# Weight buffers of an expert layer: eight in place of four, and the loads of the early tiles moved to its start

## The chip, the cores and the metric

The kernel runs on one core of one Trainium2 chip. The metric is the device time of one execution in microseconds (us), the median of several runs. A difference of 0.2%, about 4 us here, is about the smallest that these runs can tell from none.

## The reference, cut to what matters

Two transformer-like layers work on 4096 tokens of width D = 256, each an attention-like part and a mixture of experts, each with a residual and a layer norm:

```python
x = _layernorm(x + _L0_attn_ref(...))   # three recurrent (RG-LRU) layers
x = _layernorm(x + _L0_ffn_ref(x, Wg, W1, W2))   # 8 experts, each token goes to one
x = _layernorm(x + _L1_attn_ref(...))   # attention, 16 heads, 512 tokens a row
x = _layernorm(x + _L1_ffn_ref(...))   # 16 experts, each token goes to four
```

The change is in the second line, whose expert part is

```python
cap = max(1, T // E)                       # T = 4096, E = 8, cap = 512
_, top_idx = jax.lax.top_k(pT, cap)        # each expert takes its 512 best tokens
...
for e in range(E):
    gate = jnp.where(tok2exp == e, weights, 0.0)
    h = jax.nn.gelu(xt @ W1[e], approximate=False) @ W2[e]
    out = out + gate[:, None] * h
```

W1 is 256 x 512 and W2 512 x 256 for each expert, all in float32.

## The kernel before, in words

**Stages.** `block` (L1846) runs the recurrent layers, the first expert layer (`expert_choice_layer`, L1119), the attention (`attention_layer`, L1522) and the second expert layer (`token_choice_layer`, L1789) one after the other. A scheduler places the instructions of each engine, except in regions marked `manual_schedule`, where the named engines keep the order of the program.

**The first expert layer.** Each token's row is written to the list of its expert in device memory (`m0rows`) by an indirect DMA from POOL, 128 rows at a time (`put`, L729, L731). The lists are cut into tiles of 128 rows, which are worked one by one: 39 tiles, a number that covers every way in which the tokens may fall. The first eight, the early tiles (`NE0` = 8, L47), are full tiles made from the first half of the tokens. They need only the first half of the list writes: POOL issues 19 of its 32 writes, then a fence (`fence`, L746, a memset at L749 that waits for 16 of them), then the gathers of the eight early tiles (`gather`, L878, L882), with the remaining writes between them.

A table in SBUF (`table`, L770) tells for each tile where its rows start, which expert's weights it needs, and whether the expert differs from that of the table's entry before. Tiles t, t+4, t+8 and so on are given adjacent entries of the table (`entry`, L841), so that they mostly share an expert. SP reads these entries into registers (`value`, L849, L851).

**Weights.** One tile's weights are one DMA of 128 x 2068 floats, 1034 KB (`weights`, L920). The kernel has NW = 4 weight buffers, and tile t uses buffer t % 4. Tiles 0 to 3, and 8 to 11 (the first four of the second table), are loaded without a condition (L925). All others are conditional DMAs (L927), which move nothing if the buffer already holds the right expert. A load into a buffer waits until PE is done with the buffer's last tile.

**The tile loop of `run` (L898).** For tile t, `turn` transposes the rows on PE (L943) and copies them on DVE (L945); `first` multiplies by W1 on PE (L956) with the gelu on ACT (L964); `second` multiplies by W2 on PE (L978), after which DVE adds the residual (L1202) and POOL scatters the rows to `res` (L1205), two scatters under way at most. After `second(t-1)` SP loads the rows of tile t+3 (L935) and then its weights. In this layer SP and POOL keep the order of the program; PE, ACT and DVE don't have to.

SP's order at the start is: the weights of tiles 0 to 3 (L985); eight DMAs that end the lists (`end_list`, L758, L765); the table entries of tiles 4 to 7, read ahead (L989); nothing for the rows of tiles 0 to 7, which were gathered; the weights of tile 4, 5, 6 and 7, one in each turn of the loop; the rows and weights of tile 8, and so on. The rows of tile 8 need all list writes (`L.close`, L1196). At the end of the layer eight DMAs bring `res` back to SBUF (L1224), once the last scatters have landed.

**What follows.** The attention begins with a layer norm (L59 and following) of those eight parts, transposes (L143), the values V (L1566, with the weights `wv`, loaded at L1548) and their bias (L1587, with the table `bt`, loaded at L1550). Its pools of SBUF reuse the bytes of the expert layer's released pools; a pool is given by default to wait for every user of a released pool on whose bytes it lands.

The second expert layer uses the same class, with `bias` True; there the number of buffers and the order of the loads stay as they are.

Of the kernel before, what the change touches and what calls it, by code (L numbers as in the profile page):

```python
# [10 lines left out]
F32 = mybir.dt.float32  # L11
# [6 lines left out]
P = 128  # L18
# [29 lines left out]
NW = 4  # L48
G1 = S // P
WPK = DC * F + FC * D + FC + E1  # L50
# [636 lines left out]
class Lists:  # L687
# [82 lines left out]
    def table(self, n, up, t0, done=None):  # L770

        nc, rp, E, nm = self.nc, self.rp, self.E, f"{self.name}_{t0}"
        tab = rp.tile([P, 4], I32, name=f"tab{nm}")
        self.tabs.append((t0, tab))
        nb_i = rp.tile([P, E], I32, name=f"nb_i{nm}")
        nb = rp.tile([P, E], F32, name=f"nb{nm}")
        cum = rp.tile([P, E], F32, name=f"cum{nm}")
        le = rp.tile([P, E], F32, name=f"le{nm}")  # L780
        et = rp.tile([P, 2], F32, name=f"et{nm}")
        blk = rp.tile([P, 1], F32, name=f"blk{nm}")
        more = rp.tile([P, 1], F32, name=f"more{nm}")
        self.nb, self.cum = nb, cum

        def blocks():
            nc.vector.tensor_scalar_add(nb_i, n, float(up))
            nc.vector.tensor_single_scalar(nb_i, nb_i, 7, ALU.logical_shift_right)
            nc.vector.tensor_copy(nb, nb_i)
            if done is not None:  # L790
                nc.vector.tensor_sub(nb, nb, done)

        def ends():
            nc.vector.tensor_tensor_scan(cum, self.ones[:, :E], nb, 0.0, ALU.mult, ALU.add)
            nc.vector.tensor_scalar(
                le, cum, self.pnw, None, ALU.is_le, ALU.add, accum_out=et[:, 1:2]
            )
            nc.vector.tensor_scalar(
                le, cum, self.pno, None, ALU.is_le, ALU.add, accum_out=et[:, 0:1]
            )  # L800

        def block():
            nc.vector.scalar_tensor_tensor(le, le, 1.0, nb, ALU.mult, ALU.mult, accum_out=blk)
            nc.vector.tensor_sub(blk, self.pno, blk)
            if done is not None:
                nc.vector.tensor_scalar(le, self.iot, et[:, 0:1], None, ALU.is_equal)
                nc.vector.scalar_tensor_tensor(
                    le, le, 1.0, done, ALU.mult, ALU.mult, accum_out=more
                )
                nc.vector.tensor_add(blk, blk, more)  # L810

        def entries():
            nc.vector.tensor_scalar_mul(blk, blk, float(P))
            nc.vector.scalar_tensor_tensor(blk, et[:, 0:1], float(LT), blk, ALU.mult, ALU.add)
            nc.vector.tensor_scalar_min(tab[:, 0:1], blk, float(E * LT))
            nc.vector.tensor_scalar(
                tab[:, 1:2], et[:, 0:1], float(P), float(E * P - P), ALU.mult, ALU.min
            )

            nc.vector.tensor_tensor(tab[:, 2:3], et[:, 0:1], et[:, 1:2], ALU.not_equal)  # L820

        return [(0.8, blocks), (0.7, ends), (0.6, block), (0.8, entries)]
# [26 lines left out]
    def value(self, t, n, hi):  # L849
        i, tab = self.entry(t), self.of(t)[1]  # L850
        return self.nc.values_load_multi_w_load_instructions(  # L851
            tab[i : i + 1, n : n + 1],
            engines=[mybir.EngineType.SP], min_val=0, max_val=hi,
            skip_runtime_bounds_check_because="clamped where the table is made",
        )[1][0]
# [32 lines left out]
    def weights_of(self, t, w_pack):  # L888
        at = self.value(t, 1, self.E * P - P)
        return w_pack.rearrange("e p f -> (e p) f")[bass.ds(at, P), :]  # L890
# [7 lines left out]
    def run(self, ctx, ident, w_pack, bias, done, taken=None, besides=None):  # L898

        tc, nc, E, NT, nm = self.tc, self.nc, self.E, self.NT, self.name
        table, value, weights_of = self.of, self.value, self.weights_of
        wp = ctx.enter_context(tc.tile_pool(name=f"{nm}w", bufs=1))
        hp = self.hp
        psX = ctx.enter_context(tc.tile_pool(name=f"{nm}psX", bufs=2, space=PSUM))
        psH = ctx.enter_context(tc.tile_pool(name=f"{nm}psH", bufs=4, space=PSUM))
        psO = ctx.enter_context(
            tc.tile_pool(name=f"{nm}psO", bufs=1 if bias else 2, space=PSUM)
        )  # L910
        ws = [None] * len(self.held) + [
            wp.tile([P, WPK], F32, name=f"{nm}ws{i}") for i in range(len(self.held), NW)
        ]
        ws[: len(self.held)] = self.held
        xgs, hTs, read = {}, {}, {}

        def known(t):
            return weights_of(t, w_pack), None if t - table(t)[0] < NW else value(t, 2, 1)

        def weights(t):  # L920
            if t < len(self.held):
                return
            w, differs = read.pop(t, None) or known(t)
            if differs is None:
                nc.sync.dma_start(ws[t % NW], w)  # L925
            else:
                nc.sync.dma_start(ws[t % NW], w, cond=differs)  # L927

        def load(t):
            if t in self.got:  # L930
                xgs[t] = self.got.pop(t)
                return
            xgs[t] = hp.tile([P, RW], F32, tag="xg", bufs=NW + 1, name=f"{nm}xg_{t}")
            at = value(t, 0, E * LT)
            ins = nc.sync.dma_start(xgs[t], self.rows[bass.ds(at, P), :]).ins  # L935
            if t < self.early:
                self.reads(ins)

        def turn(t):
            xg = xgs[t]  # L940
            ps = psX.tile([P, DC, P], F32, tag="x", name=f"{nm}xp_{t}")
            for dc in range(DC):
                nc.tensor.transpose(ps[:, dc, :], xg[:, dc * P : (dc + 1) * P], ident)  # L943
            xq = hp.tile([P, DC, P], F32, tag="xq", name=f"{nm}xq_{t}")
            nc.vector.tensor_copy(xq, ps)  # L945
            xgs[t] = (xg, xq)

        def first(t):
            xg, xq = xgs[t]
            w = ws[t % NW]  # L950
            hT = hp.tile([P, FC, P], F32, tag="hT", name=f"{nm}hT_{t}")
            for fc in range(FC):
                ps = psH.tile([P, P], F32, tag="h", name=f"{nm}h_{t}_{fc}")
                for dc in range(DC):
                    o = dc * F + fc * P
                    nc.tensor.matmul(  # L956
                        ps, w[:, o : o + P], xq[:, dc, :],
                        start=(dc == 0), stop=(dc == DC - 1),
                    )
                o = DC * F + FC * D + fc  # L960
                if bias:
                    ins = nc.scalar.activation(hT[:, fc, :], ps, AF.Gelu, bias=w[:, o : o + 1])  # L962
                else:
                    ins = nc.scalar.activation(hT[:, fc, :], ps, AF.Gelu)  # L964
            hTs[t] = hT
            if taken:
                taken(t, xg, w)
                xgs[t] = None, None
            return ins.ins

        def second(t):
            xg, _ = xgs.pop(t)
            hT = hTs.pop(t)
            w = ws[t % NW]
            ps = psO.tile([P, D], F32, tag="o", name=f"{nm}o_{t}")
            for fc in range(FC):
                o = DC * F + fc * D
                nc.tensor.matmul(  # L978
                    ps, hT[:, fc, :], w[:, o : o + D], start=(fc == 0), stop=(fc == FC - 1)
                )  # L980
            done(t, xg, ps)


        for t in range(0 if bias else NW):
            weights(t)  # L985
        if besides:
            besides(-1, None)

        read.update({t: known(t) for t in range(NW, 0 if bias else self.early)})  # L989
        for t in range(NW):  # L990
            load(t)
            if bias:
                weights(t)
        turn(0)
        for t in range(NT + 1):
            if t < NT:
                ins = first(t)
            if t + 1 < NT:
                turn(t + 1)
            if t > 0:  # L1000
                second(t - 1)
                if t + NW - 1 < NT:
                    load(t + NW - 1)
                    weights(t + NW - 1)
            if besides and t < NT:
                besides(t, ins)

# [951 lines left out]
```

## Time and profile before

| What | Value |
|---|---|
| Timed runs (3) | median 1981.51 us, 1978.31 to 1982.03 |
| Profiled execution | 1997.18 us, of which 1995.4 us span |
| Granted TensorE clock, mean of the span | 0.928 |
| PE busy | 1738.8 us (87%) |
| DVE, ACT, POOL busy | 1131.7, 1003.7, 523.9 us |
| First expert layer: first weight load issued, last matmul over | 472.4 us, 665.7 us |
| Weight loads issued in it | 39, 1034 KB each |
| Early tiles' gathers issued by POOL | 495.5 to 515.2 us |

The profile is of one execution, and times in it count from its span's start. In a timeline a row is one instruction or a merged run of them: start, length, engine, line, what is written and read, how many; in brackets how long the engine sat idle before it and what ended that. PE is the matmul row of TensorE, PEld its weight loads, SPq the DMA issues of SyncE. A row of DMA_DIRECT2D has the issue's length on its engine, not that of the transfer.

### The profile page before, as it was taken

What the parts mean: (1) busy time and instruction counts of PE and PEld (TensorE: products, weight loads), DVE (VectorE), ACT (ScalarE), POOL (GpSimd) and SP (SyncE); (2) the same over time, 40 slices, a digit from 0 to 9 for tenths busy, and PEclk for the clock granted to TensorE, in tenths of its full rate; (3) what the DMA queues carried; (4) which work ended last, traced back from release to release, by engine and by line L of the source; (5) the groups of instructions that cost most, each with busy time, mean ns of one, the idle gap of its engine ahead of it and who ended that gap; (6) DMA issues with size and microseconds to landing.
All of it is one profiled execution on the core that took longest, in us unless ns stands there. A gap on an engine that the chain in (4) does not pass through costs nothing. (4 is left out here: it accounts for less than half of the span.)

```text
span 1995.4 us, 31137 instructions
## 1 busy us (share of the span) xinstructions
PE 1738.8 (87%) x10398; PEld 1137.1 (57%) x10398; DVE 1131.7 (57%) x2844; ACT 1003.7 (50%) x2166; POOL 523.9 (26%) x447
## 2 busy tenths in 40 slices
PE   7999995531799698898989998987999999999995
PEld 3555553321699585222222222323889999999994
DVE  6999998853122541676877786884434222222226
ACT  4899976400123331357666766655534334343343
POOL 1000000004422221001041323243666644444440
PEclk8999998655799897899999999998999999999998
DMA  9990000004554300000010111122676767566558
GB/s 358 399 390 1 1 0 1 32 7 166 178 187 147 121 1 17 16 17 17 16 59 17 59 34 43 43 84 73 162 211 130 152 158 186 110 145 139 118 103 255
DMA packets 115262, 217.10 MB, mean 109 GB/s; under 512 B 17101, under 2 KB 85919, under 8 KB 108320
## 3 DMA queue, kind: packets, MB, share of 16 engines
q1 hardware_dynamic: 81536, 165.77, 25.3%
q0 software_dynamic: 30560, 46.72, 11.8%
q10 hardware_dynamic: 3008, 2.63, 0.4%
q8 instruction: 84, 1.38, 0.3%
q14 instruction: 74, 0.61, 0.1%
HBM read 244.79 MB, written 100.43 MB: 173 GB/s over the span
## 5 line engine op out<-in xcount | busy, mean ns | idle before, releaser
L1758 DVE TENSOR_REDUCE nmx<-s 128x1 f32<-128x512 f32 x512 | 330.0, 686 | 157.9 <-PE t L1680 98.7
L1765 ACT ACTIVATE pe<-t 128x512 f32<-128x512 f32 x512 | 277.8, 594 | 206.7 <-PE t L1680 195.0
L1668 PE MATMUL s<-kT,qT 32*128 32x512 f32 x1024 | 302.8, 665 | 54.2 <-ACT pe L1765 25.6
L1680 PE MATMUL t<-qA,kT 32*128 32x512 f32 x1024 | 291.3, 645 | 2.5 <-ACT pe L1765 2.0
L1817 POOL DMA_INDIRECT acc<-y,at x143 | 221.7, 1550 | 260.0 <-DVE at L1810 192.5
L1668 PEld LDWEIGHTS s<-kT,qT 32*128 32x128 f32 x1024 | 81.6, 189 | 219.7 <-ACT pe L1765 174.5
L962 ACT ACTIVATE m1hT<-m1h,m1ws 128x128 f32<-128x128 f32 x284 | 103.9, 368 | 154.9 <-PE m1h L956 133.9
L962 ACT ACTIVATE m1hT<-m1h,xT 128x128 f32<-128x128 f32 x288 | 105.6, 368 | 148.8 <-PE m1h L956 131.5
L1816 DVE TENSOR_SCALAR y<-m1o,gt 128x256 f32<-128x256 f32 x143 | 69.1, 483 | 169.6 <-PE m1o L978 163.2
L945 DVE COPY m1xq<-m1xp 128x256 f32<-128x256 f32 x143 | 60.6, 424 | 180.2 <-PE m1h L956 87.8
L731 POOL DMA_INDIRECT m1rows<-x_ext,slot x128 | 127.0, 992 | 114.5 <-ACT pe L1765 74.8
L956 PE MATMUL m1h<-m1xq,xT 128*128 128x128 f32 x1152 | 143.4, 278 | 4.6 <-issue 2.9
L956 PEld LDWEIGHTS m1h<-m1xq,xT 128*128 128x128 f32 x1152 | 141.2, 194 | 9.3 <-issue 3.8
L956 PEld LDWEIGHTS m1h<-m1xq,m1ws 128*128 128x128 f32 x1136 | 137.4, 192 | 7.0 <-issue 3.5
L956 PE MATMUL m1h<-m1xq,m1ws 128*128 128x128 f32 x1136 | 138.7, 275 | 2.4 <-DVE m1xq L945 2.3
L978 PE MATMUL m1o<-xT,m1hT 128*128 128x256 f32 x576 | 138.4, 382 | 0.7 <-issue 0.5
L1704 PE MATMUL po<-pe,V 128*17 128x512 f32 x1024 | 136.4, 605 | 1.2 <-ACT pe L1765 1.2
L978 PE MATMUL m1o<-m1ws,m1hT 128*128 128x256 f32 x568 | 134.9, 379 | 0.0
L1734 POOL TENSOR_TENSOR AO<-AO,on 128x256 f32<-128x256 f32 x32 | 23.5, 735 | 352.6 <-DVE on L1729 335.0
L964 ACT ACTIVATE m0hT<-m0h 128x128 f32<-128x128 f32 x156 | 43.2, 278 | 143.8 <-PE m0h L956 117.6
L978 PEld LDWEIGHTS m1o<-xT,m1hT 128*128 128x128 f32 x576 | 104.3, 192 | 12.3 <-ACT m1hT L962 0.7
L978 PEld LDWEIGHTS m1o<-m1ws,m1hT 128*128 128x128 f32 x568 | 102.2, 190 | 10.8
(358 smaller groups left out, 3005.7 us busy)
## 6 DMA issues: line engine op xcount, KB each, us to landing
xT<-in_w_pack SPq DMA_DIRECT2D x72, 1034.0 KB
m1ws<-in_w_pack SPq DMA_DIRECT2D x71, 1034.0 KB
m0ws<-in_w_pack SPq DMA_DIRECT2D x39, 1034.0 KB
m0rows<-zero SPq DMA_DIRECT2D x5, 6360.0 KB
m1xg<-m1rows SPq DMA_DIRECT2D x143, 138.0 KB
acc<-zero SPq DMA_DIRECT2D x2, 4096.0 KB
f<-acc SPq DMA_DIRECT2D x16, 512.0 KB
m0rows<-zero SPq DMA_DIRECT2D x1, 4770.0 KB
```

What stands on the lines that cost most here:

```text
L731: ins = self.nc.gpsimd.indirect_dma_start(out=self.rows[:, :], out_offset=bass.IndirectOffsetOnAxis(ap=place, axis=0), in_=row, in_offset= ...
L945: nc.vector.tensor_copy(xq, ps)
L956: nc.tensor.matmul(ps, w[:, o : o + P], xq[:, dc, :], start=(dc == 0), stop=(dc == DC - 1),)
L962: ins = nc.scalar.activation(hT[:, fc, :], ps, AF.Gelu, bias=w[:, o : o + 1])
L978: nc.tensor.matmul(ps, hT[:, fc, :], w[:, o : o + D], start=(fc == 0), stop=(fc == FC - 1))
L1668: mm = nc.tensor.matmul(ps, qTs[u % NR][r, qc * P : (qc + 1) * P], kTs[u % NR][r, :], start=True, stop=True,)
L1680: mm = nc.tensor.matmul(ps, kTs[v % NR][r, kc * P : (kc + 1) * P], qAs[v][r, :], start=True, stop=True,)
L1704: mm = nc.tensor.matmul(po[h4 * HP : h4 * HP + VW, :], V[:, b * NQ + kc, 4 * g + h4, :], pes.pop((u, kc, h4)), start=(kc == 0), stop=(kc = ...
L1758: ins = nc.vector.tensor_reduce(at, ps, AX.X, ALU.max, negate=True)
L1765: ins = nc.scalar.activation(pe, ps, AF.Exp)
L1816: nc.vector.tensor_scalar_mul(y, ps, gt)
L1817: nc.gpsimd.indirect_dma_start(out=R.acc[t % 2][:, :], out_offset=bass.IndirectOffsetOnAxis(ap=at, axis=0), in_=y, in_offset=None, compute ...
```

## The change

For this layer the number of weight buffers becomes eight, the number of early tiles. Tile t up to 7 has buffer t; from tile 8 on it is t % 4 as before. The weights of tiles 4 to 7 are loaded without a condition, right behind the DMAs that end the lists, ahead of the loop; in the loop the loads begin with tile 8. Their read-ahead of conditions goes away. The second expert layer keeps four buffers.

```diff
         ws = [None] * len(self.held) + [
-            wp.tile([P, WPK], F32, name=f"{nm}ws{i}") for i in range(len(self.held), NW)
+            wp.tile([P, WPK], F32, name=f"{nm}ws{i}")
+            for i in range(len(self.held), NW if bias else self.early)
         ]
...
-        xgs, hTs, read = {}, {}, {}
+        xgs, hTs = {}, {}
+
+        many = 0 if bias else self.early
+        at = lambda t: t if t < many else t % NW
 
         def known(t):
-            return weights_of(t, w_pack), None if t - table(t)[0] < NW else value(t, 2, 1)
+            return weights_of(t, w_pack), None if t < many or t - table(t)[0] < NW else value(t, 2, 1)
 
         def weights(t):
             if t < len(self.held):
                 return
-            w, differs = read.pop(t, None) or known(t)
+            w, differs = known(t)
             if differs is None:
-                nc.sync.dma_start(ws[t % NW], w)
+                nc.sync.dma_start(ws[at(t)], w)
             else:
-                nc.sync.dma_start(ws[t % NW], w, cond=differs)
+                nc.sync.dma_start(ws[at(t)], w, cond=differs)
...
-            w = ws[t % NW]
+            w = ws[at(t)]
...
         if besides:
             besides(-1, None)
-
-        read.update({t: known(t) for t in range(NW, 0 if bias else self.early)})
+        for t in range(NW, many):
+            weights(t)
         for t in range(NW):
             load(t)
...
                 if t + NW - 1 < NT:
                     load(t + NW - 1)
-                    weights(t + NW - 1)
+                    if t + NW - 1 >= many:
+                        weights(t + NW - 1)
```

More of the change, by code (lines that the diff above doesn't have):

```diff
@@ L973, in second @@
             hT = hTs.pop(t)
-            w = ws[t % NW]
+            w = ws[at(t)]
             ps = psO.tile([P, D], F32, tag="o", name=f"{nm}o_{t}")
```

## The prediction

> **What bounds the kernel now.** The page's chain that ended last covers only the tail, so I read the first expert layer (472 to 668 us of the profiled execution) by itself, first as a table of stages. Columns after the stretch: its length, busy us (count) of PE, PEld, DVE, ACT and POOL, granted TensorE clock, DMA share, GB/s.
>
> ```profile
> 476.00:492.00 16.00, 0.00 (x0) 0.00 (x0) 0.00 (x0) 1.28 (x1) 12.35 (x13) 0.50 1.03 390
> 492.00:496.00 4.00, 0.00 (x0) 0.00 (x0) 0.00 (x0) 0.00 (x0) 0.63 (x3) 0.50 0.62 181
> 496.00:516.00 20.00, 14.63 (x72) 12.86 (x72) 1.27 (x3) 2.22 (x8) 15.43 (x16) 0.69 0.33 106
> 516.00:528.00 12.00, 0.72 (x3) 0.75 (x4) 1.30 (x3) 1.00 (x4) 6.32 (x8) 0.60 0.51 170
> ...
> 536.00:556.00 20.00, 20.00 (x143) 18.97 (x143) 4.10 (x10) 6.57 (x24) 4.99 (x6) 1.00 0.96 351
> 556.00:664.00 108.00, 108.00 (x753) 102.02 (x753) 26.35 (x58) 32.02 (x116) 29.23 (x30) 1.00 0.42 136
> 664.00:668.00 4.00, 1.73 (x8) 1.17 (x7) 0.97 (x2) 1.56 (x2) 0.97 (x1) 1.00 0.09 33
> ...
> 672.00:684.00 12.00, 6.03 (x17) 4.30 (x18) 7.88 (x34) 5.63 (x12) 0.00 (x0) 0.50 1.05 333
> ```
>
> From 536 to 664 PE is never idle at full clock: tiles 4 to 38 are bound by TensorE, and no weight load is late for it. Time can only change ahead of that (the head, 472 to 536) or behind it (the hand-over to attention, 664 to 700). Next, the timeline of the head (start, length, engine, line; idle time before and its releaser in brackets):
>
> ```profile
> 491.10 0.98 POOL L731 DMA_INDIRECT m0rows<-x_ext,slot  x1 [0.30 <-issue]
> 494.66 0.10 POOL L749 MEMSET m0full<- 128x1 f32 x1 [2.58 <-DMA m0rows<-x_ext,slot]
> 495.54 1.05 POOL L882 DMA_INDIRECT m0got<-m0rows,at  x1 [0.78 <-POOL m0full L749]
> ...
> 498.62 0.66 PE L943 MATMUL m0xp<-ident,m0got 128*128 128x128 f32 x2 [25.48 <-DMA m0got<-m0rows,at]
> ...
> 516.11 19.81 SPq L927 DMA_DIRECT2D m0ws<-in_w_pack  x4
> ...
> 527.28 3.75 PE L956 MATMUL m0h<-m0xq,m0ws 128*128 128x128 f32 x16 [11.36 <-ACT m0hT L964]
> ```
>
> The layer starts when the last list write ahead of the fence lands (494.66) and then the first gather (498.6): two small transfers in series. Weights of tiles 0 to 3 were issued at 472.4 to 475.6 and are not what PE waits for. The four conditional loads of tiles 4 to 7 go out only at 516.1 to 535.9; the waits of SP say why (total, times, longest):
>
> ```profile
> SPq L927 <- PE m0o L978: 21.3, 1, 21.3
> ```
>
> That 21.3 us is SP waiting for tile 0's buffer, with nothing behind it that PE needs: first(4) starts at 535.83, when tile 4's weights (issued 516.11) are long there, and PE is busy without a break from 528. It is a long wait that costs nothing.
>
> **The change part by part.** (1) Removed: four reads of the condition on SP (the eight reads of that moment have a median of 0.60 us) and SP's wait. SP is not late here, so 0; if it were, 4 x 0.6 = 2.4 us.
>
> (2) Moved: the loads of tiles 4 to 7 go from 516 to 536 to right behind the eight end-of-list writes (SP is done with those at 489.5), so about 490.5 to 494. In before one of the four was skipped: of the four issues the shortest took 113 ns against 333 to 359 for the others, the time of an issue that moves nothing. So the change moves 4 x 1034 KB = 4.24 MB at once, 1.06 MB of it new. At 390 GB/s less what POOL's own list writes take (138 KB per 1.28 us, 110 GB/s) that is 280 GB/s, some 15 us: the DMA stays full until about 506, where before it fell to a share of 0.62 at 492 and 0.33 from 496. Into exactly that stretch fall the last list writes, the fence and the first gathers.
>
> What does a full queue cost a small indirect transfer? Two rows of the same kind, a tile's 128 KB scatter:
>
> ```profile
> 534.40 0.97 POOL L1205 DMA_INDIRECT res<-z,m0got  x1 [5.58 <-DVE z L1202]
> ...
> 541.17 0.97 POOL L1205 DMA_INDIRECT res<-z,m0got  x1 [3.73 <-DMA res<-z,m0got]
> ...
> 666.53 0.97 POOL L1205 DMA_INDIRECT res<-z,m0xg  x1 [2.54 <-DVE z L1202]
> 668.93 7.48 SPq L1224 DMA_DIRECT2D x_ext<-res  x8
> ```
>
> The scatter at 541.17 waits for the one two before it, issued at 534.40: 6.8 us with weights in the queue. The last one (666.53) releases SP at 668.93: 2.4 us with the queue empty. So a full queue adds 4.4 us. In the head the gather took 498.5 - 495.5 = 3.0 us, so up to 3.8 more; the last list write took 3.56 us, partly under load already, so up to 3.2 more. Upper bound 7.0 us; lower bound 0 (more bytes in the queue can't make a write land sooner). The Trainium skill (DMA: Bandwidth & Descriptors, Queues, rings and completion order) says that each DMA engine takes turns between its queues packet by packet. By that rule a 138 KB transfer still gets half of 390 GB/s and loses only 0.35 us, 0.7 us for the two; by the scatter's row it is 7.0. The row is of this kernel, but had two weight loads and a backlog ahead; I take +1.5 for the fence and +2.5 for the gather, **+4**. All of it moves PE's start and nothing later absorbs it, since PE is the bound from then on.
>
> (3) Buffers: tiles 8 to 11 now reuse buffers 0 to 3, free long before, so their loads need only the fence at 537.3 and no longer tile 4 to 7. PE was not waiting (20.00 of 20.00 busy at 536 to 556), so 0.
>
> (4) Bytes of SBUF, which the diff doesn't show. In the program before, the weight pool lies at bytes 134,080 to 167,216 of each partition (8,288 a buffer); eight buffers end at 200,368. The attention layer's `wv` (from 176,160) and `bt` (to 188,448) then lie on buffers 5 and 6. All tiles of a pool wait for every user of the released pools on whose bytes it lands. Before, those two loads were clear of the layer and ran ahead of it:
>
> ```profile
> L1548 SPq DMA_DIRECT2D wv<-in_Wv x1: 380/380/380, 391.8 to 391.8; - x1
> ...
> L1550 SPq DMA_DIRECT2D bt<-in_bt x1: 467/467/467, 392.2 to 392.2; - x1
> ```
>
> while `wq` and `wk`, which do lie on the layer's bytes, went out at 684. After, `wv` and `bt` (256 + 1280 KB = 1.57 MB) must wait for tile 38's last matmul (663.83 + 1.89 = 665.7). SP is then idle until 668.93, so I expect them at once, ahead of the eight `x_ext<-res` loads. 1.57 MB at 333 to 390 GB/s is 4.0 to 4.7 us. The idle DMA of 665.7 to 668.9 (share 0.09) hides 3.2 us of it, leaving 0.8 to 1.5; but the last scatter, which gates the res loads, now shares a full queue (0 to +4.4 us). From 672 to 684 the DMA is full (1.05), so a delay there is passed on to the first layer norm at 673.26 and to PE behind it. Bounds +0.8 and +5.9; with the transfer's 1 and about a fifth of the scatter's 4.4, **+2**. A gain from their absence at 391 is excluded: the gates then wait for the end of the recurrent layers (402.9), not for a DMA.
>
> Sum: 0 + 4 + 0 + 2 = +6 us on the profiled execution's own 1997.18 (span 1995.4 and 1.8 around it). The timed runs have a median of 1981.51, 15.7 us shorter; the profile's PE gaps at 508 to 527 (2.1 and 11.4 us, ended late although the work ahead was recorded as done) may be longer in it than in timed runs. They contain no wait for weights, so the sum doesn't use them: 1981.5 + 6 = **1987.5 us**.
>
> **The rivals.** *Faster: the gap at 516 to 527 is the load's doing.* Tile 4's load, issued at 516.11, fills the DMA (share 0.81 at 516 to 520) just when the last gathers and list writes are under way, and PE resumes only at 527. With the load gone from there PE could resume earlier by between the load's own 4.7 us (1.06 MB at the 224 GB/s of 516 to 520) and the whole gap of 11.4; I take 6, and 2 back for the hand-over: 1977.5. It decides from the point where the gap shrinks by more than the two small delays, 6 us. Against it: PE's instruction there waits for ACT, not for a DMA, and the gap outlasts the load. *No change: the loads are hidden.* The share of 0.33 at 496 to 516 has room for them, the skill's rule holds (+0.7), and the hand-over costs 0.8 to 2: 1983.5. *Worse: SP's order.* If `wv` and `bt` come behind `krow` (685.0), V's first matmul moves from 680.1 to about 688; PE then has 43 busy us to do in a stretch of 47, so 5 to 8 us are lost instead of 2: 1992.
>
> **How the numbers follow.** The likeliest case, both small delays (1983 to 1990), has 0.53; SP's order 0.11; no change 0.21; faster 0.15. Differences within 0.2% (4 us: 1977.5 to 1985.5) are what a measurement of this kernel can't tell from none. Slower than that: 0.49 of the likeliest and SP's 0.11, together 0.60; same: the 0.21, 0.04 of the likeliest and 0.05 of the faster case, 0.30; faster by more, 0.10. The range reaches about to the middle of the faster case, 1978, and past SP's order with the upper bounds of both delays, 1995.
>
> **What would show it.** Right: four weight issues at 490 to 495; a DMA share near 1 until about 505; fence at 496, first gather's data for PE at 502 to 503; the same 3.8 us a tile from then on; `wv` and `bt` at 666, `x_ext<-res` at 670, first layer norm at 675. Wrong: PE's first matmul still at 498.6 (then the skill's rule holds); PE's gap at 516 to 527 gone or longer; `wv` still at 391.

## The result and the profile after

The kernel before has a median of 1980.45 us (20 runs, 1973.89 to 1984.64), the changed one 1988.78 us (20 runs, 1981.81 to 1993.1). The ratio is 1.0034, with a 95% interval of 1.0024 to 1.0044: 6.7 us slower (4.8 to 8.7). The two medians by themselves are 8.3 us apart; the ratio, which has the interval, is used from here on. The profiled execution after took 1992.7 us (span 1990.9). It can't be set against the profiled 1997.18 us of before: that one lies far outside the runs that it was shown with (1978.31 to 1982.03), and the section on the experiments comes back to it.

The table of stages of after, columns as in the prediction:

```profile
492.00:496.00 4.00, 0.00 (x0) 0.00 (x0) 0.00 (x0) 0.00 (x0) 0.06 (x1) 0.50 1.09 230
496.00:516.00 20.00, 11.67 (x73) 10.90 (x74) 2.18 (x5) 3.33 (x12) 14.56 (x16) 0.70 0.78 302
516.00:528.00 12.00, 12.00 (x84) 11.23 (x83) 3.45 (x8) 3.34 (x12) 8.66 (x10) 1.00 0.34 115
```

The DMA share of 492 to 516 has risen from 0.62 and 0.33 to 1.09 and 0.78: the four loads are there. PE begins later (11.67 us busy in the 20 us instead of 14.63), but the gap of 516 to 528, where PE had 0.72 us of work in 12, is gone. That last difference isn't the change's doing, as the experiments will show. The timeline of the head of after:

```profile
490.22 3.62 SPq L929 DMA_DIRECT2D m0ws<-in_w_pack  x4
496.39 0.10 POOL L749 MEMSET m0full<- 128x1 f32 x1 [4.34 <-DMA m0rows<-x_ext,slot]
497.27 1.05 POOL L882 DMA_INDIRECT m0got<-m0rows,at  x1 [0.78 <-POOL m0full L749]
...
503.48 0.66 PE L947 MATMUL m0xp<-ident,m0got 128*128 128x128 f32 x2 [30.33 <-DMA m0got<-m0rows,at]
```

The fence comes 1.7 us later than before (494.66), and the gather takes 503.5 - 497.3 = 6.2 us instead of 3.1. PE starts 4.9 us later. The hand-over to attention in the timeline of after:

```profile
651.66 1.89 PE L982 MATMUL m0o<-m0ws,m0hT 128*128 128x256 f32 x8
...
653.58 0.40 SPq L1553 DMA_DIRECT2D wv<-in_Wv  x1
654.02 0.46 SPq L1555 DMA_DIRECT2D bt<-in_bt  x1
654.35 0.97 POOL L1210 DMA_INDIRECT res<-z,m0xg  x1 [2.54 <-DVE z L1207]
660.04 6.95 SPq L1229 DMA_DIRECT2D x_ext<-res  x8
...
664.12 1.41 DVE L59 BATCH_NORM_STATS2 st_m<-x_ext 128x6 f32<-128x256 f32 x4 [3.50 <-DMA x_ext<-res]
...
668.61 2.17 PE L143 MATMUL tp<-ident,x_ext 128*128 128x128 f32 x8 [15.07 <-ACT x_ext L68]
```

`wv` and `bt` have moved from 391.8 to right behind tile 38's last matmul (653.55). The last scatter shares the DMA with them and needs 660.04 - 654.35 = 5.7 us instead of 2.4 until it releases SP. From the last matmul to the first layer norm it is 10.6 us instead of 7.5, and PE's idle time ahead of the first attention transposes (the bracket of the last row) is 15.07 us. Before it was this:

```profile
677.40 2.17 PE L143 MATMUL tp<-ident,x_ext 128*128 128x128 f32 x8 [11.67 <-ACT x_ext L68]
```

### The profile page after: what moved, and what is told of

Its sections match the earlier page's. It is cut to its first block, busy times and chain, and to the rows that moved or that the text cites. A ratio compares the mean times of both kernels' runs of the same rounds, so it can differ in the third digit from the quotient of the medians.

```text
span 1990.9 us, 31138 instructions
## 1 busy us (share of the span) xinstructions
PE 1741.2 (87%) x10398; PEld 1136.8 (57%) x10398; DVE 1130.9 (57%) x2844; ACT 1003.8 (50%) x2166; POOL 523.5 (26%) x447
## 4 chain that ended last, share of the span: by engine, by line
PE 54%; DVE 4%; ACT 4%; issue 2%; POOL 1%; DMA 1%; SPq 0%; ACTq 0%; POOLq 0%; DVEq 0%
PE s L1673 13%; PE m1h L960 13%; PE m1o L982 12%; PE po L1709 5%; PE qk L1645 3%; PE bv L1592 2%; DVE nmx L1763 2%; ACT pe L1770 2%; PE m1xp L947 2%; PE v L1571 1%; PE t L1685 1%; ACT L99 1%; ACT L98 1%; DVE st_m L59 1%; DMA acc<-y,at 0%
```

## The experiments

Theory A is the prediction's: a delay of PE's start (4 to 5 us) and one of the hand-over (2 to 3) add up. Rivals: B, all in the head; C, all in the hand-over; D, the extra megabyte, the missing condition or the order of the instructions.

**Each place undone, and one alone.** `tail_undone` moves the attention's small pool clear of the eight buffers:

```diff
+            pad = pre.enter_context(tc.tile_pool(name="avpad", bufs=1))
+            hole = pad.tile([P, 6144], F32, name="hole")
             vp = pre.enter_context(tc.tile_pool(name="av", bufs=1))
```

> The change, with a hole of 24,576 bytes ahead of the attention layer's pool for wv and bt, so that they lie behind the eight buffers (from byte 200,736) and are loaded at 391 us again. Theory A (both places): the head's delay stays, the hand-over's goes: 4 to 5 us over the kernel before, 2 to 3 under the change; in the profile wv at 391, the last scatter landing 2.4 us after its issue, first gather's data still 6 us after its issue. Rival B (all of the loss in the head): 7 us over the kernel before. Rival C (all in the hand-over): 0. Rival D (the 1.06 MB and the eight buffers themselves): 7.

`tail_alone` is the kernel before with eight buffers reserved, of which it uses four:

```diff
-            wp.tile([P, WPK], F32, name=f"{nm}ws{i}") for i in range(len(self.held), NW)
+            wp.tile([P, WPK], F32, name=f"{nm}ws{i}")
+            for i in range(len(self.held), NW if bias else self.early)
```

> The kernel before, with eight buffers reserved of which four stay unused, so that only the bytes move: wv and bt have to wait for the layer's last matmul, and every weight load is as before. Theory A: 2 to 3 us over the kernel before, the last scatter landing about 5.7 us after its issue instead of 2.4. Rival B: 0. Rival C: 7. Rival D: 0 if it is the megabyte.

`head_undone` is the change with the early loads behind the first rows; `both_undone` has the hole as well:

```diff
-                nc.sync.dma_start(ws[at(t)], w)
+                ins = nc.sync.dma_start(ws[at(t)], w).ins
+                if t == NW and not bias:
+                    tc.add_manual_dep(ins, self.gathers[NW - 1].name, SYNC, reason="rows first")
```

> The change, with tile 4's load held on SP until the fourth gather has landed (5 to 7 behind it): all four unconditional and early, but behind the first rows; the hand-over as in the change. Theory A: the fence at 494.7 and PE's first transpose at 498.6 again, 2 to 3 us over the kernel before, 4 to 5 under the change. Rival B: 0 over before. Rival C: 7 over before. Rival D: 7 over before.

> Both of these together: eight buffers and four unconditional loads stay, but they are issued behind the fourth gather, and wv and bt lie clear of the layer. Theory A, B and C: the time of the kernel before within 1.5 us. Rival D (the extra megabyte, the missing condition, or the order of the instructions): 7 us over it still.

Measured against the kernel before on the same chip (median 1993.38 us there), with the 95% interval: `tail_undone` 1.0003 (0.9990 to 1.0015), +0.6 us; `tail_alone` 1.0041 (1.0028 to 1.0053), +8.2; `head_undone` 1.0036 (1.0026 to 1.0046), +7.2; `both_undone` 1.0007 (0.9992 to 1.0022), +1.4. On this chip that is rival C: moving the bytes alone costs all of the loss, and undoing the head brings nothing. D falls, since `both_undone` keeps the megabyte, the missing condition and the order. In the timeline of `tail_alone`, where no weight load differs from before:

```profile
664.63 0.40 SPq L1548 DMA_DIRECT2D wv<-in_Wv  x1
665.08 0.46 SPq L1550 DMA_DIRECT2D bt<-in_bt  x1
665.40 0.97 POOL L1205 DMA_INDIRECT res<-z,m0xg  x1 [2.54 <-DVE z L1202]
...
672.69 0.33 POOL L723 MEMSET m1none<- 128x276 f32 x1 [6.32 <-DMA res<-z,m0xg]
...
681.27 2.17 PE L143 MATMUL tp<-ident,x_ext 128*128 128x128 f32 x8 [16.68 <-ACT x_ext L68]
```

The scatter takes 7.2 us, and PE's idle time is 16.68 us, 5.0 more than before. But in `tail_undone` the head is as late as in after (first transposes at 502.61), and the time is that of before. Where does the head's delay go?

**PE's gap.** PE's start moved by 4 us and the end of its gap didn't: PE is back for good at 528.14 in `tail_undone`, at 527.28 in before. In the gap it waits for ACT, and ACT for PE's results. The waits of ACT from 496 to 530, in before (total us, times, longest):

```profile
ACT m0hT L964 <- PE m0h L956: 28.9, 7, 24.1
ACT m0hT L964 <- remote: 17.3, 4, 11.0
```

"Remote" is a wait that no recorded end of work explains. Two rows of before show the longest of them:

```profile
510.28 2.46 PE L956 MATMUL m0h<-m0xq,m0ws 128*128 128x128 f32 x16 [2.09 <-ACT m0hT L964]
...
521.01 0.28 ACT L964 ACTIVATE m0hT<-m0h 128x128 f32<-128x128 f32 x1 [11.02 <-remote]
```

PE's matmuls by W1 are over at 512.7, and ACT begins its gelu of them only at 521.0, 8.3 us later. All this time POOL issues list writes and gathers back to back. Theory E: the gap ends with POOL's stream, whenever PE began, so the head's delay is lost in it. `after_again` is the change itself on another chip of this kind. `lists_first` moves POOL's later list writes ahead of the first gather, so PE starts much later and has less of the stream beside it:

```diff
-            put(NC // 2 + 3)
+            put(left)
             L.grown = L.fence(NC // 2)
             for t in range(NE0):
                 L.gather(t)
-                if t >= NW - 1:
-                    put(min(left, 2))
-            put(left)
```

> The change itself, on the chip of the four runs before. Theory A (head and hand-over add up): 7 us by the hand-over and 4 to 5 by the head, 11 to 12 over the kernel before. Theory E (on this chip PE has a gap of about 13 us in the first tiles, which ends with POOL's list writes whenever PE began, so that the head's delay is lost in it): 6 to 8 us, all of the hand-over; in the profile PE starts at 503 but is at tile 10 at the time of the kernel before, within 1.5 us.

> The kernel before, with POOL's 13 later list writes put ahead of the first gather: weights, conditions and bytes as before; PE's first tile starts 13 x 1.3 = 17 us later. Theory E: PE runs with no gap then, and 13.5 of the 17 us are regained: 2 to 5 us over the kernel before. Theory A (a delay of PE's start is a delay of the layer): 17 us over.

Against the kernel before (1995.89 us there): `after_again` 1.0025 (1.0013 to 1.0036), +5.0 us; `lists_first` 1.0026 (1.0017 to 1.0035), +5.2 us. PE's first transposes in `lists_first` are at 510.82, 12.2 us later than in before's profile, and its first W2 matmul 19.3 us later. The rest of its gap ends behind the last gather:

```profile
517.02 1.00 POOL L882 DMA_INDIRECT m0got<-m0rows,at  x1 [0.30 <-issue]
519.79 0.71 PE L956 MATMUL m0h<-m0xq,m0ws 128*128 128x128 f32 x4 [2.74 <-issue]
523.30 2.08 PE L956 MATMUL m0h<-m0xq,m0ws 128*128 128x128 f32 x8 [2.80 <-ACT m0hT L964]
```

A is refuted for such a chip: it wanted +11 to 12 for `after_again` and +17 for `lists_first`, and even the 12.2 us by which PE's start really moved are more than twice the measured 5.2. E wanted 6 to 8 and 2 to 5, and both intervals reach into these.

**What of the hand-over costs.** `bt_behind` lets only `wv` ahead of the rows; `tail_dose` doubles `bt`:

```diff
-            nc.sync.dma_start(bt, a["bt"].rearrange("p (k y) -> p k y", k=NQ))
+            late = nc.sync.dma_start(bt, a["bt"].rearrange("p (k y) -> p k y", k=NQ)).ins
+            tc.add_manual_dep(late, a["rows_in"][-1].name, SYNC, reason="rows first")
```

> The change, with the load of bt (1280 KB) held until the last of the eight x_ext<-res loads has landed; wv (256 KB) stays where the change puts it, and the bytes too. If the hand-over's loss is the DMA time of wv and bt ahead of the rows, 1.31 of 1.57 MB of it goes: 1 to 3 us over the kernel before instead of 7, with the last scatter landing 3 us after its issue. If it is the wait itself, or the order of the attention layer's instructions: 7 us still.

```diff
-            bt = vp.tile([P, NQ, 20 * 32], F32, name="bt")
-            nc.sync.dma_start(bt, a["bt"].rearrange("p (k y) -> p k y", k=NQ))
+            twice = vp.tile([P, 2, NQ * 20 * 32], F32, name="bt")
+            nc.sync.dma_start(twice, a["bt"].unsqueeze(1).to_broadcast([P, 2, NQ * 20 * 32]))
+            bt = twice[:, 0, :].rearrange("p (k y) -> p k y", k=NQ)
```

> The change, with bt loaded in two copies by one transfer (2560 KB), so that 2.88 MB stand ahead of the rows instead of 1.57. If the loss is DMA time: 1.31 MB at 340 to 390 GB/s, 3.4 to 3.9 us more than the change, 10 to 12 over the kernel before, and the last scatter lands some 9 us after its issue. If it is the wait: as the change.

`bt_behind` 1.0001 (0.9985 to 1.0017), +0.2 us: with the bytes where the change puts them and only `bt`'s transfer moved, the loss is gone. So it is the DMA time of `bt` and neither the wait nor the bytes as such. `tail_dose` 1.0041 (1.0028 to 1.0054), +8.2 us (5.6 to 10.8), is 3.2 more than the change beside it (2.6 to 7.2); that agrees, but the intervals overlap, and 10 to 12 were expected. The timeline of `bt_behind`:

```profile
660.89 0.40 SPq L1555 DMA_DIRECT2D wv<-in_Wv  x1
661.66 0.97 POOL L1210 DMA_INDIRECT res<-z,m0xg  x1 [2.54 <-DVE z L1207]
664.20 7.29 SPq L1230 DMA_DIRECT2D x_ext<-res  x8
...
673.01 2.16 PE L143 MATMUL tp<-ident,x_ext 128*128 128x128 f32 x8 [12.15 <-ACT x_ext L68]
...
680.66 0.43 SPq L1557 DMA_DIRECT2D bt<-in_bt  x1
```

The scatter is back at 2.5 us and PE's idle time at 12.15 us. In `tail_dose` the scatter took 6.5 us, not the 9 expected; the other bytes met the row loads, and PE's idle time was 17.09 us.

**A shorter stream.** If the gap ends with POOL's stream, fewer gathers there should make the kernel faster. `gathers_4` (and with 0 in place of 4 `gathers_0`) is before, with

```diff
             for t in range(NE0):
-                L.gather(t)
+                if t < 4:
+                    L.gather(t)
```

`early_gathers_4` is the same in `tail_undone`.

> The kernel before, with only tiles 0 to 3 gathered by POOL; the rows of tiles 4 to 7 come by plain loads from SP's queue. POOL's stream of list writes and gathers is 4 x 1.3 = 5.2 us shorter; PE's start is as before. Theory E (PE's gap ends 3 to 5 us behind the end of POOL's stream): PE is back at 522 instead of 527, and the kernel is 3 to 5 us faster than before. Theory A (the gap has nothing to do with POOL's stream): the time of the kernel before.

> The kernel before, with no gathers on POOL: all eight early tiles' rows come by plain loads from SP's queue. POOL's stream is 8 x 1.3 = 10.4 us shorter. Theory E: PE is back at about 517, and the kernel is up to 10 us faster, less what SP's eight reads and loads cost ahead of the first tile (0.6 us each, 1 to 3 us at the start, which the gap hides). Theory A: the time of before or slower by those 1 to 3 us.

> The change with the bytes of wv and bt clear of the layer (the hole of the first run) and only four gathers on POOL: eight unconditional loads, no loss at the hand-over, a shorter stream. Theory E: as the same without the change, 3 to 5 us faster than the kernel before, since the head's delay is still lost in what is left of the gap (8 of 13 us). Theory A: 4 to 5 us slower than before, by the head.

Against before (1997.27 us there): `gathers_4` 1.0008 (0.9997 to 1.0018), `gathers_0` 1.0005 (0.9992 to 1.0017), `early_gathers_4` 1.0026 (1.0013 to 1.0038), +5.2 us. The gap did what E said; this is `gathers_4`, with the last list write and PE's return:

```profile
515.44 0.97 POOL L731 DMA_INDIRECT m0rows<-x_ext,slot  x1 [0.30 <-issue]
519.98 2.02 PE L956 MATMUL m0h<-m0xq,m0ws 128*128 128x128 f32 x16 [0.52 <-ACT m0hT L964]
```

Yet no time came of it, and the expected gains were missed. In `gathers_0` the first layer norm is at 664.48, 7.5 us ahead of that of `both_undone` (671.93), but the attention's first score matmul is not (772.42 and 772.37). Here is the stretch a little behind the layer norm's start, in `gathers_0` and then in `both_undone`:

```profile
680.00:688.00 8.00, 4.77 (x21) 3.35 (x20) 7.88 (x18) 2.37 (x5) 4.89 (x3) 0.80 0.00 0
688.00:696.00 8.00, 7.86 (x28) 5.27 (x28) 7.35 (x26) 5.80 (x12) 0.99 (x1) 0.77 0.00 1
```

```profile
684.00:692.00 8.00, 7.84 (x43) 6.52 (x42) 7.82 (x24) 4.99 (x11) 4.31 (x2) 1.00 0.36 95
692.00:700.00 8.00, 5.52 (x26) 3.84 (x25) 7.80 (x22) 5.22 (x11) 4.99 (x3) 0.93 0.00 1
```

DVE, the third engine of a row, is nearly full in both, so it is not what makes `gathers_0` slower here. The granted clock differs (0.80 and 0.77 against 1.00 and 0.93), but each is one execution. Why the time saved ahead of attention is lost behind it stays open.

`early_gathers_4` was expected to gain and lost 5.2 us. Its first layer norm is at 672.54, 5.4 us behind `gathers_4` (667.12), so the shorter stream no longer hid the head's delay. But that is only 1.2 us behind `tail_undone` (671.32), which costs nothing, so the length of the layer alone doesn't explain its loss either.

**A small shift ahead of attention.** The trace's record of the granted clock has half-clock stretches of 3.41 us or multiples, and attention's length follows them. From its first score matmul to the second expert layer's first matmul, before and `after_again` (the columns end with PEclk, DMA share, GB/s):

```profile
777.17:1391.82 614.65, 553.76 (x3620) 163.52 (x3620) 439.07 (x1002) 373.35 (x690) 136.82 (x129) 0.96 0.13 37
```

```profile
777.85:1398.71 620.86, 559.83 (x3620) 164.73 (x3620) 438.90 (x1000) 373.60 (x691) 136.81 (x129) 0.95 0.12 36
```

Does a small delay of attention cost more than itself by this? `shift` is before with

```diff
+            idle = psV.tile([P, 2, D], F32, tag="o", name="idle")
+            for j in range(4):
+                nc.tensor.matmul(
+                    idle[:, j % 2, :], xT[:, 0, :P], wv[:, 0, :], start=True, stop=True
+                )
```

> The kernel before, with four matmuls of 128x256 more (their result unused) between the bias matmuls and the attention's first q/k matmul, 4 x 0.23 = 0.9 us on PE at full clock; nothing else is changed. It asks whether a small delay ahead of attention costs more than itself. In the profiles so far the clock is granted in stretches of multiples of 3.41 us, and attention took 614.7 us with 54 us of half clock in it where its first score matmul stood 2.65 us into such a stretch, and 620 to 621 us with 64 to 68 us where it stood at 3.2 or at 0.1. Theory P (the start's place in the grid is fixed by the program): the place moves from 2.65 to 0.1 to 0.2, and the kernel is 5 to 7 us slower. Theory L (the place falls differently in each execution, or doesn't matter): 0.9 us slower, within the noise.

1.0004 (0.9992 to 1.0015), +0.8 us: theory L, though the four matmuls took 1.89 us in its profile and not 0.9. Its first score matmul stood at 3.25 us in the grid, not at 0.1, and attention took 615.4 us, against 620.9 in `after_again`, which stood at 3.2. So the place in the grid is not fixed by the program and doesn't by itself set attention's length. One thing stays open: attention took 614.7 to 618.0 us in the six profiles with before's weight loads and 617.9 to 620.9 in the eight with the change's. Two of the six are the fastest executions of their kernels (`tail_alone`, `gathers_0`), so this may be chance in what was profiled, but that the change has no part in it is not shown.

This run brought more than that. The kernel before had 1981.59 us on its chip, as in the first comparison, and the profile of `shift`, which is that of before up to attention, has none of this gap; PE's one pause is 4.23 us long and waits for rows:

```profile
497.21 0.66 PE L943 MATMUL m0xp<-ident,m0got 128*128 128x128 f32 x2 [24.74 <-DMA m0got<-m0rows,at]
...
506.29 9.75 SPq L927 DMA_DIRECT2D m0ws<-in_w_pack  x4
...
513.82 1.04 POOL L882 DMA_INDIRECT m0got<-m0rows,at  x1 [0.30 <-issue]
...
520.12 0.66 PE L943 MATMUL m0xp<-ident,m0got 128*128 128x128 f32 x2 [4.23 <-DMA m0got<-m0rows,at]
```

and ACT has no "remote" wait in it:

```profile
ACT m0hT L964 <- PE m0h L956: 45.6, 24, 23.4
```

So the record has two kinds of chips: some where the kernel before takes about 1981 us, with no such gap in the two profiles from them (`shift` and after), and some with 1993 to 1997 us and a gap of 9 to 14 us with the order of POOL's work as it was. By its time and its gap, the profile of before that the prediction read looks like one of the second kind; its timed runs were of the first, like the runs and the profile of after. And the rows above say what becomes of the head's delay on the first kind: the eighth gather, issued by POOL at 513.82 while the conditional loads are under way (DMA share 0.90 at 514 to 518, 1.01 at 518 to 522), lands at 520.1, and PE stands 4.23 us for tile 7's rows. In after PE is later by then and the loads are over, and it doesn't stand.

**All runs together.** Starts of the attention's first score matmul in each profile, beside the time over before (us, from the ratios):

| Kernel | First score matmul | PE idle ahead of L143 | Over before |
|---|---|---|---|
| chips of 1993 to 1997 us | | | |
| both_undone | 772.37 | 11.12 | +1.4 (-1.6 to 4.4) |
| tail_undone | 773.30 | 11.22 | +0.6 (-2.0 to 3.0) |
| bt_behind | 771.51 | 12.15 | +0.2 (-3.0 to 3.4) |
| gathers_4 | 770.32 | 12.20 | +1.6 (-0.6 to 3.6) |
| gathers_0 | 772.42 | 12.27 | +1.0 (-1.6 to 3.4) |
| early_gathers_4 | 776.50 | 12.27 | +5.2 (2.6 to 7.6) |
| lists_first | 777.60 | 11.41 | +5.2 (3.4 to 7.0) |
| tail_alone | 775.91 | 16.68 | +8.2 (5.6 to 10.6) |
| head_undone | 777.69 | 15.29 | +7.2 (5.2 to 9.2) |
| after_again | 778.04 | 15.17 | +5.0 (2.6 to 7.2) |
| tail_dose | 781.28 | 17.09 | +8.2 (5.6 to 10.8) |
| chips of 1981 us | | | |
| shift | 761.62 | 11.15 | +0.8 (-1.6 to 3.0) |
| after | 767.32 | 15.07 | +6.7 (4.8 to 8.7) |

On the second kind, the kernels level with before start the scores by 773.3, the slower ones behind 775.9. Two single executions don't fit this and keep it from being more than support: before's own, with 777.17, would stand among the slow ones, and `tail_alone`'s took 1992.8 us, 8.5 less than the median of its 19 runs. The start of `shift` has its 1.9 us of added matmuls in it.

## Why the prediction was right, and where it was not

The forecast (+6 us; measured +6.7) was right by its sum, and that was luck: its term for the head was some 3 us too large, its term for the hand-over some 2 to 6 us too small, and the two errors cancelled.

**Removed condition and wait: 0.** Holds: `both_undone`, without either, is no faster than before (+1.4, interval across zero).

**Moved loads, +4.** What was foreseen at the place itself came: the issues at 490.2 to 493.8, fence +1.7 (foreseen 1.5; 2.4 against `shift`), gather +3.1 (2.5). What failed is the step "all of it moves PE's start and nothing later absorbs it, since PE is the bound from then on". On the first kind of chip, measured from a fixed matmul ahead of the layer, PE's first W1 matmul in after comes 5.9 us later than in `shift`, its last tile's transposes only 1.3 us later: 4.5 us are taken back, which fits the 4.23 us that PE no longer stands for tile 7's rows. On the second kind PE's gap takes it: `tail_undone` costs 0.6 us (-2.0 to 3.0). The prediction saw that gap and set it aside as perhaps peculiar to its profile; it should have asked what ends it. In `early_gathers_4`, with less cover, the delay is not lost within the layer, but what that costs in time is not clear.

**The estimate of +0.7 us for both,** drawn from the packet-by-packet turns that the Trainium skill describes (DMA: Bandwidth & Descriptors, Queues, rings and completion order), was far too low: fence and gather lost 4.9 us together, and the scatter of the hand-over, 2.4 us alone, took 5.7 to 7.2 us beside `wv` and `bt`. Whether the turns are taken so can't be seen in these traces; the step from them to half the bandwidth is what failed.

**Earlier buffers: 0.** Nearly: after has two waits for weights, of 0.4 us each, at 537 and 545, since the loads of tiles 8 to 10 go out together at 531 to 536; before's PE was busy for all 20 us of 536 to 556.

**Bytes of SBUF, +2.** The place was right (`wv` and `bt` follow the layer's last matmul at once) and on the second kind of chip it is the whole cause: `tail_alone` gives the loss with nothing else changed. The transfer's own 1 us didn't show: from the release of SP to the first layer norm it is 4.1 us in after and 4.3 in before. The mis-sized term is the scatter's. It was taken at a fifth of its 4.4 us; it came at 3.3 us in after, 3.3 in `after_again`, and 4.8 in `tail_alone`, which is above the bound. PE's idle time rose by 3.4 to 5.0 us. The timed runs ask for 5.0 to 8.2 us, with intervals of 2 to 3 us either way. Whether 1 to 3 us more are lost behind the first transposes stays open: V and attention scatter by as much from one execution to the next. Over all timed runs the mean granted clock is 0.931 in before, 0.928 in `tail_alone` and in `head_undone`, so part of the loss may be clock.

On the first kind of chip no run undid one place alone. There the terms are, from `shift` to after: 1.3 us by the head, 3.9 by the hand-over and 1.1 from the first transposes to the last bias matmul, together 6.3 beside the measured 6.7. Each is the difference of two single profiles, and these two differ by 9.0 us in all, 3.4 of them in attention.

**The rivals.** "The gap is the load's doing" falls for the gap that it names: in `tail_undone` no weight load is issued near 516 and the gap is there; in `shift` four loads are issued from 506 to 516 and there is none. But its mechanism, a load that collides with the last gathers, fits the 4.23 us in `shift`; on that kind of chip the pause is gone with the change, much as the rival said, and only about makes up for the head's delay. "No change" was half right: the loads in the head are nearly hidden. SP's order didn't come: `wv` and `bt` stood ahead of `krow`.

## What to carry to other kernels

More buffers move whatever is allocated on the bytes behind them: look up which later loads then have to wait, because a transfer that was free early in the kernel can come back in the narrowest place, here 1.57 MB between the last scatter and the rows that attention waits for. A delay ahead of a busy engine counts only as far as that engine never waits again before the end of the stage; look for the next wait, and for what ends it. And check that the profiled execution is like the timed ones before working with its gaps. No version here beat the kernel before; the change with `bt` held back, or with its bytes moved, is level with it.

## What the runs showed of the hardware that was not expected

- While POOL issued indirect DMAs back to back, ACT and DVE took up PE's results late on some chips (8.3 us in the rows above; such waits of ACT add up to 17.3 us in before's profile) and not on others. Chips with this have a kernel median 12 to 16 us longer (1981 against 1993 to 1997 us), but that the gap is what makes them slower is not shown: `gathers_4` and `gathers_0` shortened it and gained nothing. That the late start is due to POOL's stream is supported by the gap's end, which moved with the stream (528 in `after_again`, 520 in `gathers_4`, 523 in `lists_first`, where only gathers were left); why chips differ is open.
- The granted clock changes in steps of 3.41 us that don't start with the kernel: the same first matmul stood anywhere in the step. The Trainium skill (TensorE: Matmul & The Clock Gate, Part 1) calls this window free-running, which these traces bear out: the first score matmul stood 0.1 us into a step in `early_gathers_4`, 1.0 in `lists_first`, 1.9 in `both_undone` and 3.25 in `shift`.
- A 128 KB scatter took 2.4 us with a nearly idle DMA (share 0.09), 5.7 to 7.2 us beside 1.57 MB and 6.5 us beside 2.88 MB.
